# Two of a residual stream's additions as accumulating transfers within SBUF, in a four-layer graph network

## The chip, the cores and the metric

The kernel runs on one core of a Trainium2 chip. A core has five engines that run their own instruction queues and wait for each other by semaphores: TensorE (PE in the profile), VectorE (DVE), ScalarE (ACT), GpSimd (POOL) and SyncE (SP, which here only issues transfers). Sixteen DMA engines move data between HBM and SBUF and within SBUF. The metric is the device time of one execution in microseconds (us); less is better. Before the change it is 2353.62 us, the median of three runs from 2353.39 to 2353.85 us.

## The reference

There are 32 graphs of 512 nodes with 256 features. Each goes through four layers of the form x = x + layer(relu(layernorm(x)), adj), all in float32:

```python
# layer 0: att = softmax(h @ att_W @ h.T / 16 + mask)
#          y = tanh(att @ (h @ W0 + b0));  z = tanh(att @ (y @ W1 + b1));  x = x + z
# layer 1: e = leaky_relu(src + dst), masked; x = x + softmax(e) @ (h @ W.T)
# layer 2: e = exp(-leaky_relu(s + d)) where adj; x = x + elu(e @ (h @ W) / rowsum(e))
# layer 3: e = leaky_relu(h' a_12 h'.T + ...), masked; x = x + elu(h @ W_1 + (softmax(e) @ h) @ W_2)
```

The sums "x + z" of layer 0 and "x + elu(...)" of layer 2 are where the change lies. elu(v) is computed as relu(v) + min(exp(v), 1) - 1, so layer 2 has two additions to x per block.

## The kernel before

**Tiles.** A graph's x is one SBUF tile of 128 partitions by 4 blocks of 256 float32 (512 KB). Work on it goes in two halves, g = 0 and 1, of two blocks each: 128 x 512 elements, 256 KB. One graph at a time goes through the layers, but up to six graphs are in flight, each at another layer, so that PE always has matmuls of some graph to do. All big tiles share one pool of 34 "pages" of 4 KB per partition; the eight PSUM banks are shared too.

**The order.** It is written out by a planner inside the kernel (class `Plan`). Every step is registered with `op(engine, cost, after, emit, ...)`: its engine ("PE", "V" for DVE, "A" for ACT, "G" for GpSimd, "D" for transfers issued by SP), a pair of costs (how long it holds its engine, and after how long its result can be used), and what it comes after. `order` then lays the steps out by list scheduling: at each moment an engine takes the ready step with the earliest due time, where due times follow from the graph's number times a spacing and from the costs of what is still to come. A step with a `size` is booked with a shared wire instead: its bytes divided by 200 bytes per ns, plus 2000 ns. `best` tries 64 pairs of spacings and keeps one. The order that results is fixed in the program; on the chip each engine runs its queue strictly in that order and waits where a semaphore isn't there yet. The spacings chosen are 32000 and 8000 before, 34000 and 8000 after.

**Around layer 0's addition** (lines 936 to 952). For each half: eight matmuls give two blocks in one bank (`second_conv`, L936); two DVE instructions scale them and add the bias into z (`biased`, L940); ACT takes the tanh in place (`tanh2`, L944); DVE adds z to x (`add_z`, L947). Layer 1's normalisation (`normed`) starts from x: DVE takes statistics of each block (L557, L558), DVE and GpSimd make the factors (L561, L564, L567), ACT normalises (L571), the result goes through a transposing transfer issued by SP and back through ACT into hT (L591), and from there to PE.

**Around layer 2's additions** (lines 999 to 1018). For each block ACT writes exp into y2 (`lower`, L999) and relu into r2 (`upper`, L1002). For each half DVE adds min(y2, 1) to x (`add_lower`, L1009) and then r2 - 1 to x (`add_upper`, L1013). Layer 3's normalisation follows in the same way as above.

**GpSimd** does little: the reciprocal square roots for the normalisations (L564) and one 512 KB store per graph (L1154), which is a transfer issued from its queue. Its queue too is strictly in order.

Of the kernel before, what the change touches and what calls it, by code (L numbers as in the profile page):

```python
# [11 lines left out]
F32 = mybir.dt.float32  # L12
# [3 lines left out]
AF = mybir.ActivationFunctionType  # L16
ALU = mybir.AluOpType
PSUM = bass.MemoryType.PSUM

P = 128  # L20
# [13 lines left out]
def pe(n512=0, n258=0, n256=0, nt=0):  # L34
    t = n512 * PE512 + n258 * PE258 + n256 * PE256 + nt * PET
    return t, t + 170.0
# [3 lines left out]
V_MASK, V_CODE, V_HALF, V_PSUM, V_ADD = (602.0, 683.0), (600.0, 690.0), (600.0, 690.0), (395.0, 484.0), (334.0, 425.0)  # L40
A_COPY, A_HALF, A_PRELU, A_EXP, A_TANH = (477.0, 597.0), (253.0, 373.0), (570.0, 693.0), (519.0, 640.0), (373.0, 474.0)
A_BIAS, A_PRELU2 = (570.0, 687.0), (629.0, 722.0)
G_POW, G_STORE = (800.0, 850.0), (900.0, 900.0)
V_SUM, V_BLOCK = (334.0, 425.0), (790.0, 880.0)
A_HALF_BIAS = (345.0, 460.0)
A_NORM, A_JOIN, V_SPLIT = (491.0, 590.0), (620.0, 767.0), (332.0, 422.0)
# [160 lines left out]
def kernel(  # L207
# [31 lines left out]
    nc = tc.nc  # L239
    B, N, H = x.shape  # L240
# [9 lines left out]
    const = ctx.enter_context(tc.tile_pool(name="const", bufs=1))  # L250
# [69 lines left out]

    zero = const.tile([P, 1], F32, tag="zero", name="zero")
    nc.gpsimd.memset(zero, 0.0)
    one = const.tile([P, 1], F32, tag="one", name="one")
    nc.gpsimd.memset(one, 1.0)
    minus = const.tile([P, 1], F32, tag="minus", name="minus")
    nc.gpsimd.memset(minus, -1.0)

    def tile_of(name, cols, lines=HC):
        return const.tile([P, lines, cols], F32, tag=name, name=name)
# [7 lines left out]
    def raw(key, cols=H):  # L337
        return lambda: W[key][:, :, :cols]

    def load(dst, src, *keys):  # L340

        loads.append(prepare("G", G_LOAD, [], lambda: nc.gpsimd.dma_start(out=dst() if callable(dst) else dst, in_=src),
                             *keys, size=P * HC * H * 4 if keys else 4096))
        return loads[-1]

    def rows_of(w):
        return w.rearrange("(c p) k -> p c k", p=P)

    def load_column(t, v):

        return load(t, v.rearrange("(c p) -> p c", p=P))
# [5 lines left out]
    def halves(w):  # L357

        return w.rearrange("p c (i k) -> p c i k", i=2)[:, :, :, 1:]
# [19 lines left out]
    def product(dst, wT, rhs, cols, after, *keys):  # L379

        done = []
        for d in range(HC):
            key = f"bank{next(banks)}"

            def multiply(d, key):
                for c in range(HC):
                    nc.tensor.matmul(W[key][:, :cols], wT()[:, c, d * P : (d + 1) * P], rhs(c),
                                     start=(c == 0), stop=(c == HC - 1))

            def out_of(d, key):  # L390
                nc.vector.tensor_copy(dst(d), W[key][:, :cols])

            cost = pe(n256=2 * HC) if cols > P else pe(nt=2 * HC)
            a = prepare("PE", cost, after, partial(multiply, d, key), key, *keys)
            done.append(prepare("V", V_ADD, [a], partial(out_of, d, key), key, *keys))
        return done
# [28 lines left out]
    for n, dst, w, key in (("w0", w0_s, w0, "raw9"), ("att", att_s, att_w, "raw10")):  # L425
        ready[key] = [prepare("D", D_X, [], lambda w=w, key=key: nc.sync.dma_start(
            out=raw(key)(), in_=rows_of(w)), key, size=P * HC * H * 4)]
# [9 lines left out]
    a = [load(l1_sb, rows_of(l1_w), "raw0")]  # L437
# [5 lines left out]
    a = [load(lambda i=i: halves(l2_wide())[:, :, i, :], rows_of(l2_w)[:, :, i * HALF : (i + 1) * HALF], "raw12")  # L443
         for i in range(2)]
    t = transposed(lambda: halves(l2_wide()), l2_wt, a, "raw1", "raw12")
    a = t + [load_column(l2_ac, l2_a.rearrange("o n -> (o n)"))]
    a = a + product(lambda d: l2_wide()[:, d, :: HALF + 1], l2_wt,
                    lambda c: l2_ac.rearrange("p (o c) -> p c o", o=2)[:, c, :], 2, a, "raw1", "raw12")
# [3 lines left out]
    a = product(lambda d: awt()[:, d, :], a12_sb, lambda c: wt3()[:, c, :], H,  # L452
                t + [load(a12_sb, rows_of(l3_a12), "raw3")], "raw3", "raw4", "raw5")
    a = product(lambda d: m3_sb()[:, d, :], wt3, lambda c: awt()[:, c, :], H, a, "raw4", "raw5", "raw6")
# [4 lines left out]
    a = [load(lambda i=i: l3_wide()[:, :, i * (HALF + 1) : i * (HALF + 1) + HALF],  # L459
              rows_of(l3_w2)[:, :, i * HALF : (i + 1) * HALF], "raw8") for i in range(2)]  # L460
# [14 lines left out]
    def graph(b, adj_before, x_before):  # L475


        T = Tiles(b)

        def op(engine, cost, after, emit, *keys, size=0, weights=()):  # L480
            return plan.op(engine, cost, after, emit, b, T.uses(keys) + W.uses(weights), size)

        def two(g):
            return slice(2 * g, 2 * g + 2)
# [7 lines left out]
        def e(l, c):  # L492

            return T[f"e{l}_{c // 2}"][:, c % 2, :]
# [5 lines left out]
        def fetch_adj(t):  # L500
            nc.sync.dma_start(out=T["adj"][:, t, :], in_=adj[b, t * P : (t + 1) * P, :])


        got_x = [op("D", D_X, [x_before], partial(fetch_x, ts), "x", "ahead", size=P * H * 4 * (ts.stop - ts.start))
                 for ts in ([slice(t, t + 1) for t in range(NT)] if b == 0 else [slice(0, NT)])]
        got_adj = [adj_before]
        for t in range(NT):

            got_adj.append(op("D", D_ADJ, got_adj[-1:] if b else [], partial(fetch_adj, t), "adj", size=P * N * 4))
# [23 lines left out]
        for g in range(NT // 2):  # L533
            code = op("V", V_CODE, [got_adj[2 * g + 2], code], partial(classes, g), "adj", "code", "slot")
            for t in (2 * g, 2 * g + 1):
                if b:
                    coded.append(op("D", D_TURN, [code], partial(turn_code, t), "code", "codeT"))
                else:
                    key = f"bank_c{t}"
                    a = op("PE", pe(nt=NT), [code], partial(turn_code_pe, t, key), "code", key)  # L540
# [273 lines left out]
        if b == 0:  # L814

            qs, vs, es = [], [], []
            for k in range(HC):
# [7 lines left out]
                a = op("PE", pe(n512=4), hs + ready["raw10"], partial(features, k, key), key, "hT0", weights=["raw10"])  # L825
                qs.append(op("A", A_COPY, [a], lambda k=k, key=key: nc.scalar.copy(T["fa0"][:, k, :], T[key]), key, "fa0"))
            for t in range(NT):
# [7 lines left out]
                a = op("PE", pe(n256=4), [hs[t]] + ready["raw9"], partial(values, t, key), key, "hT0", weights=["raw9"])  # L835
                vs.append(op("V", V_ADD, [a], lambda t=t, key=key: nc.vector.tensor_add(
                    T["v0"][:, t, LEAD : LEAD + H], T[key][:, :H], b0_sb), key, "v0"))
            for c in range(NT):
                key = f"bank_q0{c}"

                def similar(c, key):
# [4 lines left out]
                a = op("PE", pe(n512=4), qs, partial(similar, c, key), key, "hT0", "fa0")  # L846
                a = op("A", A_COPY, [a], lambda c=c, key=key: nc.scalar.activation(
                    e(0, c), T[key], AF.Exp, scale=float(H) ** -0.5), key, f"e0_{c // 2}")
# [75 lines left out]
        a = None  # L924
        for c in range(NT):
            a = op("PE", pe(n512=4), [ys[c], a], partial(again, c), "bank_z0", "bank_z1", "y0", f"e0_{c // 2}")
        zs = [op("A", A_COPY, [a], partial(evacuate_z, k), f"bank_z{k}", "zT") for k in range(HC)]
        xs = []
        for g in range(NT // 2):
            key = f"bank_o{g}"  # L930

            def second_conv(g, key):
                for j in range(2):
                    t = 2 * g + j
                    for k in range(HC):
                        nc.tensor.matmul(T[key][:, j * H : (j + 1) * H], T["zT"][:, k, t * P : (t + 1) * P],  # L936
                                         w1_sb[:, k, :], start=(k == 0), stop=(k == HC - 1))

            def biased(t, key):
                nc.vector.scalar_tensor_tensor(T["z0"][:, t, :], T[key][:, t % 2 * H : (t % 2 + 1) * H],  # L940
                                               T["rs0"][:, t : t + 1], b1_sb, ALU.mult, ALU.add)

            def tanh2(g):
                nc.scalar.activation(T["z0"][:, two(g), :], T["z0"][:, two(g), :], AF.Tanh)  # L944

            def add_z(g):
                nc.vector.tensor_add(T["x"][:, two(g), :], T["x"][:, two(g), :], T["z0"][:, two(g), :])  # L947

            a = op("PE", pe(n256=8), zs + ready["w1"], partial(second_conv, g, key), key, "zT")
            bs = [op("V", V_PSUM, [a] + ready["b1"], partial(biased, 2 * g + j, key), key, "z0") for j in range(2)]  # L950
            a = op("A", A_EXP, bs, partial(tanh2, g), "z0")
            xs += [op("V", V_MASK, [a], partial(add_z, g), "z0", "x")] * 2


        def masked1(c):
# [20 lines left out]
        xs = attend(1, es, vs, second)  # L976
# [33 lines left out]

        def add_upper(g):
            xt = T["x"][:, two(g), :]
            nc.vector.scalar_tensor_tensor(xt, T["r2"][:, two(g), :], -1.0, xt, ALU.add, ALU.add)  # L1013

        us, xs = attend(2, es, vs, third), []
        for g in range(NT // 2):
            a = op("V", V_MASK, [u[0] for u in us[two(g)]], partial(add_lower, g), "y2", "x")
            xs += [op("V", V_MASK, [a] + [u[1] for u in us[two(g)]], partial(add_upper, g), "r2", "x")] * 2

# [73 lines left out]
        a = op("V", (334.0, 425.0), hi, highest, "crest3")  # L1095
        a = op("D", D_TURN, [a], partial(turn, 0, 2), "crest3")
        a = op("V", (900.0, 1000.0), [a], tops, "crest3")
        a = op("D", D_TURN, [a], partial(turn, 1, 0), "crest3")
# [29 lines left out]
            return op("V", V_PSUM, [a, wb[0, t // 2], wb[1, t // 2]], both_terms, key, "y3", "w3")  # L1128

        def upper3(ts):  # L1130
            nc.vector.scalar_tensor_tensor(T["x"][:, ts, :], T["y3"][:, ts, :], -1.0, T["x"][:, ts, :], ALU.max, ALU.add)

        def exp4(ts):
            nc.scalar.activation(T["r3"][:, ts, :], T["y3"][:, ts, :], AF.Exp, bias=one)

        def all_terms(ts):
            nc.vector.scalar_tensor_tensor(T["y3"][:, ts, :], T["r3"][:, ts, :], 1.0, T["x"][:, ts, :], ALU.min, ALU.add)
# [4 lines left out]
        us = attend(3, es, vs, fourth)  # L1142
        last = []
        for ts in parts(3):
            ts = slice(ts[0], ts[-1] + 1)
            whole = ts.stop - ts.start == 2
            u = op("V", V_MASK if whole else V_ADD, us[ts], partial(upper3, ts), "y3", "x")
# [13 lines left out]
    for b in range(B):  # L1161
        code, got = graph(b, code, got_x[-2])
        got_x.append(got)
# [37 lines left out]
```

## Time and profile before

| What | Value |
|---|---|
| Median of three runs | 2353.62 us |
| Span of the profiled execution | 2353.1 us |
| PE busy | 2328.9 us, 99% |
| DVE busy | 2099.7 us, 89% |
| ACT busy | 1719.9 us, 73% |
| POOL busy | 254.2 us, 11% |
| Transfers issued by POOL (queue q0) | 18.23 MB, 2.4% of the DMA engines' time |
| Transfers issued by SP (queue q1) | 157.51 MB, 31.2% of the DMA engines' time |
| 512 KB store issued by POOL, issue to landing, median | 3.6 us |

The profiled execution's span is 0.5 us below the median of the runs, so sums made against the span can be read against the median directly. The busy times are sums over instructions; DVE and ACT instructions that follow each other overlap by about 0.08 us in the records, so that a 0.68 us instruction takes 0.60 us of its engine's time from start to start. Idle time of an engine matters only if the engine that sets the end waits for it.

### The profile page before, as it was taken

The page shows a single profiled execution, that of the slowest core. Times are in us where ns is not written, and L with a number is a line of the kernel's source. Part 1 is how long each engine was busy: PE and PEld are TensorE (multiplying, and loading weights), DVE is VectorE, ACT ScalarE, POOL GpSimd, SP SyncE. Part 2 cuts the span into 40 slices and gives each one's busy share as a digit, 9 for nine tenths or more (in the row PEclk, how much of TensorE's full clock was granted, in tenths as well). Part 3 has the DMA queues.
Part 4 walks back from the last instruction along what each step waited for, and adds up shares of the span by engine and source line. Part 5 has one row for each costly group of instructions (what it writes and reads, how often), then busy time and mean ns, then how long its engine had stood idle before and what let it go on. Part 6 is the DMA issues. An engine that isn't in the chain of part 4 may idle for free.

```text
span 2353.1 us, 37623 instructions
## 1 busy us (share of the span) xinstructions
PE 2328.9 (99%) x12374; PEld 1992.0 (85%) x12374; DVE 2099.7 (89%) x6060; ACT 1719.9 (73%) x3421; POOL 254.2 (11%) x316
## 2 busy tenths in 40 slices
PE   8999999999999999999999999999999999999998
PEld 5789888888888888888898888888888888888887
DVE  8788899989889898898998889989898988987998
ACT  5677778767787677786777877677776778667874
POOL 3000101111011111011110010100101000010110
PEclk9999999999999999999999999999999999999999
DMA  7431233323333332333323334233343333321221
GB/s 192 106 78 28 57 79 79 88 66 83 72 75 84 78 83 66 70 88 90 82 58 74 80 85 90 54 82 70 88 91 68 86 68 73 86 54 33 55 49 42
DMA packets 429859, 178.26 MB, mean 76 GB/s; under 512 B 384128, under 2 KB 401664, under 8 KB 429664
## 3 DMA queue, kind: packets, MB, share of 16 engines
q1 hardware_dynamic: 424288, 157.51, 31.2%
q0 software_dynamic: 5232, 18.23, 2.4%
q8 instruction: 97, 1.59, 0.3%
q14 instruction: 98, 0.80, 0.1%
q10 hardware_dynamic: 144, 0.13, 0.0%
HBM read 67.64 MB, written 16.89 MB: 36 GB/s over the span
## 4 chain that ended last, share of the span: by engine, by line
PE 94%; DVE 4%; DMA 1%; ACT 1%; issue 0%; POOL 0%; DVEq 0%; ACTq 0%
PE bank_a L758 36%; PE bank_z L918 9%; PE bank_s3p L1040 5%; PE bank_o L936 4%; PE bank_q0p L874 4%; PE bank_f3p L783 4%; PE bank_w3p L809 4%; PE bank_v0p L809 4%; PE bank_f0p L783 4%; PE bank_s3q L1040 3%; PE bank_q0q L874 3%; PE bank_v1p L809 2%; PE bank_v3p L809 2%; PE bank_v2p L809 2%; PE bank_v3q L809 2%; PE bank_v1q L809 2%
## 5 line engine op out<-in xcount | busy, mean ns | idle before, releaser
L758 PE MATMUL bank_a<-v,e 128*128 128x258 f32 (+2 forms) x4096 | 1017.7, 381 | 0.9 <-DVE e L956 0.9
L758 PEld LDWEIGHTS bank_a<-v,e 128*128 128x128 f32 x4096 | 744.1, 190 | 108.9 <-issue 18.2
L591 ACT COPY hT<-planesT 128x512 uint16<-128x512 uint16 x508 | 377.8, 769 | 93.9 <-DMA planesT<-planes 93.2
L564 POOL TENSOR_TENSOR rstd<-ve,mhalf 128x2 f32<-128x2 f32 x256 | 216.0, 863 | 1732.3 <-DVE ve L561 1599.4
L571 ACT ACTIVATE xn<-x,off,rstd 128x256 f32<-128x256 f32 x512 | 278.0, 593 | 39.8 <-DVE off L567 38.9
L918 PE MATMUL bank_z<-e,y 128*128 128x512 f32 x512 | 240.8, 593 | 0.0
L557 DVE BATCH_NORM_STATS2 st<-x 128x6 f32<-128x256 f32 x512 | 210.5, 411 | 3.8 <-DMA x<-in_x_dram 3.8
L576 DVE COPY planes<-xn 128x512 uint16<-128x512 uint16 x380 | 156.4, 420 | 17.3 <-DMA planesT<-planes 10.2
L882 ACT ACTIVATE e<-e 128x512 f32<-128x512 f32 x124 | 77.8, 629 | 121.9 <-DVE e L893 61.8
L732 ACT ACTIVATE e<-row,v 128x512 f32<-128x512 f32 x224 | 156.6, 719 | 0.8 <-DMA row<-row 0.7
L735 ACT ACTIVATE e<-e 128x512 f32<-128x512 f32 x256 | 157.1, 630 | 0.0
L918 PEld LDWEIGHTS bank_z<-e,y 128*128 128x128 f32 x512 | 92.7, 190 | 64.9 <-issue 60.5
L695 ACT COPY v<-bank_v1p 128x258 f32<-128x258 f32 x128 | 47.7, 373 | 120.0 <-PE bank_v1p L809 119.3
L936 PE MATMUL bank_o<-w_sb,zT 128*128 128x256 f32 x512 | 118.5, 379 | 0.2 <-ACT zT L922 0.2
L1047 DVE SCALAR_TENSOR_TENSOR e<-bank_s3p,v,mask 128x256 f32<-128x256 f32 x256 | 111.0, 475 | 8.4 <-PE bank_a L758 4.4
L558 DVE BATCH_NORM_AGGREGATE mv<-st 128x2 f32<-128x6 f32 x512 | 93.2, 182 | 17.5
L936 PEld LDWEIGHTS bank_o<-w_sb,zT 128*128 128x128 f32 x512 | 95.8, 190 | 12.8 <-ACT zT L922 0.6
L664 DVE TENSOR_TENSOR hs<-hT,hs 128x256 f32<-128x256 f32 x254 | 105.1, 414 | 1.1
L667 DVE TENSOR_TENSOR hs<-hT 128x512 f32<-128x512 f32 x127 | 86.6, 682 | 14.5 <-ACT hT L591 14.3
L1086 ACT ACTIVATE e<-e,zero 128x512 f32<-128x512 f32 x128 | 88.2, 721 | 12.9 <-DVE crest L1064 11.4
L885 DVE TENSOR_TENSOR e<-bank_q0p,mask 128x512 f32<-128x512 f32 x124 | 84.5, 682 | 13.8 <-PE bank_q0p L874 12.3
L1089 DVE TENSOR_TENSOR e<-e,crest 128x512 f32<-128x512 f32 x128 | 85.9, 682 | 8.3 <-ACT crest L1083 8.1
(202 smaller groups left out, 4891.3 us busy)
## 6 DMA issues: line engine op xcount, KB each, us to landing
adj<-in_adj_dram SPq DMA_DIRECT2D x128, 256.0 KB
x<-in_x_dram SPq DMA_DIRECT2D x31, 512.0 KB
out_dram<-y POOLq DMA_DIRECT2D x31, 512.0 KB, 3.6
row<-row SPq DMA_DIRECT2D x56, 256.0 KB
planesT<-planes SPq DMA_TRANSPOSE x508
codeT<-code SPq DMA_TRANSPOSE x124
crest<-crest SPq DMA_TRANSPOSE x64
row<-sT SPq DMA_DIRECT2D x56, 2.0 KB
```

Of the source, the lines that this page charges most:

```text
L557: nc.vector.bn_stats(T[f"st{l}"][:, t, :], T["x"][:, t, :])
L564: nc.gpsimd.tensor_tensor(T[f"rstd{l}"][:, two(g)], T[f"ve{l}"][:, two(g)], mhalf[:, two(g)], ALU.pow)
L571: nc.scalar.activation(T[f"xn{l}"][:, t, :], T["x"][:, t, :], AF.Relu, bias=T[f"off{l}"][:, t : t + 1], scale=T[f"rstd{l}"][:, t : t + 1])
L591: nc.scalar.copy(bits[:, :, :, t * P : (t + 1) * P], T[f"planesT{l}_{t}"].rearrange("p (b c) n -> p b c n", b=2))
L735: nc.scalar.activation(e(l, c), e(l, c), AF.Exp, scale=sign)
L758: nc.tensor.matmul(T[key][:, : LEAD + H + 1 - lead], e(l, c)[:, t * P : (t + 1) * P], T[f"v{l}"][:, c, lead:], start=(c == 0), stop=(c == ...
L783: nc.tensor.matmul(p[:, : N // 2], w[:, x - 1, :], right(x), start=fresh, stop=True, skip_group_check=True)
L809: nc.tensor.matmul(p[:, j * k : (j + 1) * k], right(x)[:, j * P : (j + 1) * P], w[:, x - 1, :], start=fresh and j == 0, stop=True, skip_gr ...
L874: nc.tensor.matmul(p[:, j * N // 2 : (j + 1) * N // 2], right(x)[:, j * P : (j + 1) * P], left(x), start=fresh and j == 0, stop=True, skip ...
L918: nc.tensor.matmul(T[f"bank_z{k}"], T["y0"][:, c, k * P : (k + 1) * P], e(0, c), start=(c == 0), stop=(c == NT - 1))
L936: nc.tensor.matmul(T[key][:, j * H : (j + 1) * H], T["zT"][:, k, t * P : (t + 1) * P], w1_sb[:, k, :], start=(k == 0), stop=(k == HC - 1))
L1040: nc.tensor.matmul(p[:, j * N // 2 : (j + 1) * N // 2], left(x)[:, j * P : (j + 1) * P], right(x), start=fresh and j == 0, stop=True, skip ...
```

## The change

In graphs 1 to 29 (graph 0 and the last two, `ends`, keep the DVE instructions), layer 0's addition and the second addition of layer 2 are no longer DVE instructions but transfers issued by GpSimd from SBUF to SBUF, each of 256 KB, with an operation that adds what is read to the destination. To the planner they are steps of engine "G" that hold it for 900 ns and have a size of 256 KB. The -1 of layer 2's elu, which the DVE instruction added on its way, is left out of x there; x is then larger by 1 everywhere until layer 3 takes it back: layer 3's normalisation doesn't see a constant, and the constants of its last terms (the bias of w3, the limit in `upper3` and the bias of the exp) change from -1, -1, 1 to -2, -2, 2. These constants change no instruction's shape. In graphs 0, 30 and 31 `add_upper` becomes a plain DVE addition of the same size.

```diff
-G_POW, G_STORE = (800.0, 850.0), (900.0, 900.0)
+G_POW, G_STORE, G_SUM = (800.0, 850.0), (900.0, 900.0), (900.0, 4500.0)
...
-    one = const.tile([P, 1], F32, tag="one", name="one")
-    nc.gpsimd.memset(one, 1.0)
-    minus = const.tile([P, 1], F32, tag="minus", name="minus")
-    nc.gpsimd.memset(minus, -1.0)
+    minus, plus = (const.tile([P, 1], F32, tag=n, name=n) for n in ("minus", "plus"))
+    nc.gpsimd.memset(minus, -2.0)
+    nc.gpsimd.memset(plus, 2.0)
...
+        ends = b < 1 or b >= B - 2
+        summed = ("V", V_MASK) if ends else ("G", G_SUM)
...
             def add_z(g):
-                nc.vector.tensor_add(T["x"][:, two(g), :], T["x"][:, two(g), :], T["z0"][:, two(g), :])
+                if ends:
+                    nc.vector.tensor_add(T["x"][:, two(g), :], T["x"][:, two(g), :], T["z0"][:, two(g), :])
+                else:
+                    nc.gpsimd.dma_start(out=T["x"][:, two(g), :], in_=T["z0"][:, two(g), :], accum_op=ALU.add)
...
-            xs += [op("V", V_MASK, [a], partial(add_z, g), "z0", "x")] * 2
+            xs += [op(*summed, [a], partial(add_z, g), "z0", "x", size=0 if ends else 2 * P * H * 4)] * 2
...
         def add_upper(g):
             xt = T["x"][:, two(g), :]
-            nc.vector.scalar_tensor_tensor(xt, T["r2"][:, two(g), :], -1.0, xt, ALU.add, ALU.add)
+            if ends:
+                nc.vector.tensor_add(xt, xt, T["r2"][:, two(g), :])
+            else:
+                nc.gpsimd.dma_start(out=xt, in_=T["r2"][:, two(g), :], accum_op=ALU.add)
...
-            xs += [op("V", V_MASK, [a] + [u[1] for u in us[two(g)]], partial(add_upper, g), "r2", "x")] * 2
+            xs += [op(*summed, [a] + [u[1] for u in us[two(g)]], partial(add_upper, g), "r2", "x", size=0 if ends else 2 * P * H * 4)] * 2
...
-            nc.vector.scalar_tensor_tensor(T["x"][:, ts, :], T["y3"][:, ts, :], -1.0, T["x"][:, ts, :], ALU.max, ALU.add)
+            nc.vector.scalar_tensor_tensor(T["x"][:, ts, :], T["y3"][:, ts, :], -2.0, T["x"][:, ts, :], ALU.max, ALU.add)
...
-            nc.scalar.activation(T["r3"][:, ts, :], T["y3"][:, ts, :], AF.Exp, bias=one)
+            nc.scalar.activation(T["r3"][:, ts, :], T["y3"][:, ts, :], AF.Exp, bias=plus)
```

In the built program, GpSimd's queue of a graph in the middle then runs: a transfer of layer 2 (half 0), two square roots of another graph, a transfer of layer 2 (half 1), two square roots, both transfers of layer 0 one after the other, three square roots, the store of an older graph and one more square root. As costs and steps have changed, the planner has laid out all engines' queues anew: PE's queue holds the same matmuls in another sequence.

## The prediction

> **What bounds the kernel now.** I read the page's busy times and the chain of work first, then the stages, then who waits for whom.
>
> ```profile
> span 2353.1 us, 37623 instructions
> PE 2328.9 (99%) x12374; PEld 1992.0 (85%) x12374; DVE 2099.7 (89%) x6060; ACT 1719.9 (73%) x3421; POOL 254.2 (11%) x316
> PE 94%; DVE 4%; DMA 1%; ACT 1%; issue 0%; POOL 0%; DVEq 0%; ACTq 0%
> ```
>
> The first two lines say that PE idles 24.2 us in all; the third, from the chain that ended last, says that the chain is PE from end to end. The stages show where the 24.2 us lie (columns: stretch, its length, busy us of PE, weight loads, DVE, ACT, POOL, granted clock, DMA share, GB/s):
>
> ```profile
> 0.00:50.00 50.00, 40.98 (x167) 27.71 (x168) 38.45 (x144) 28.27 (x53) 19.97 (x41) 1.00 0.82 206
> 50.00:100.00 50.00, 48.74 (x249) 39.62 (x248) 43.35 (x117) 30.23 (x57) 1.37 (x2) 1.00 0.52 116
> ...
> 900.00:1200.00 300.00, 299.86 (x1606) 258.46 (x1605) 271.68 (x788) 225.96 (x452) 32.15 (x38) 1.00 0.34 75
> ...
> 2100.00:2250.00 150.00, 148.18 (x820) 126.75 (x819) 130.48 (x369) 116.09 (x235) 14.46 (x16) 1.00 0.23 47
> 2250.00:2300.00 50.00, 46.06 (x240) 40.13 (x239) 47.60 (x145) 40.47 (x85) 6.29 (x7) 0.97 0.24 48
> 2300.00:2353.00 53.00, 46.61 (x266) 41.48 (x264) 46.63 (x108) 27.34 (x50) 1.51 (x2) 0.98 0.16 45
> ```
>
> From 100 to 2100 us PE is without gaps (299.86 of 300; the clock is 1.00). That its busy time there is work and not stretched by waiting shows in the timeline: twelve 259-column matmuls take 2.62 us, 0.218 us each, wherever they stand, and the same group of matmuls (L936) comes back after 288.2 us for four graphs each time, 72.05 us per graph. Of the idle time, 8.8 us pass before the first matmul, and 6.5 us after the last; no edit here touches these. Left are 8.9 us of stalls: 1.5 up to 100 us, 1.6 in the 2000 us of the middle, 1.8 from 2100 to 2250 and 3.9 from 2250 to 2300. **The change can gain 8.9 us (0.4%) at most, and only at the ends.** DVE's 89% is no bound: in the middle it is busy 271.7 of 300 us, and PE doesn't wait for it.
>
> **What the Trainium skill says.** "DMA: Bandwidth & Descriptors" (Anatomy of one DMA — SWDGE (gpsimd) path) prices a transfer issued by GpSimd at 2.0 us plus its bytes over 436 GB/s. For the 512 KB store that gives 3.2 us; the trace has 3.6, a tenth more (the view of line 1154's instructions: min/median/max of the issue in ns, then of the landing):
>
> ```profile
> L1154 POOL DMA_DIRECT2D out_dram<-y x31: 752/790/1347, 279.6 to 2345.4; - x31
> ...
> DMA to landing us min/median/max: 3.4/3.6/4.8
> ```
>
> "Collectives: The Full Stack" (The bandwidth ceiling: the fold count and why AG ≠ RS ≠ AR) says that an add in the DMA engines costs two source reads, not cycles of the adder; no run here shows that yet. "SBUF — State Buffer" (Who interferes with whom) says that a DVE copy in its two-port mode keeps GpSimd from writing descriptors; the spread of the issue, 790 ns to 1347 ns, agrees with such a delay of 0.56 us but doesn't name its cause.
>
> **The change part by part.**
>
> *Removed:* two halves of two additions in 29 graphs, 58 + 58 DVE instructions. In the groups by shape (busy us, mean ns of one, idle before it):
>
> ```profile
> L1013 DVE SCALAR_TENSOR_TENSOR x<-r,x 128x512 f32<-128x512 f32 x64 | 43.6, 681 | 0.3
> L947 DVE TENSOR_TENSOR x<-x,z 128x512 f32<-128x512 f32 x64 | 43.6, 682 | 0.4 <-ACT z L944 0.4
> ```
>
> 58 x 0.682 + 58 x 0.681 = 79.1 us, so DVE falls to about 2021 us (86%). On the path this is worth nothing in the middle, since PE covers it; cover gone, it would be 116 x 0.60 = 70 us. The constants are free: no instruction changes its shape.
>
> *Added on POOL:* 116 issues. At the store's 0.79 us they are 92 us, POOL 346 us (15%). Hidden: POOL idles over 2000 us. Its queue is in order, though: square roots (L564) now stand behind transfers that wait for a tanh or for add_lower. In the built order the roots behind a transfer are mostly of steps that come later anyway, and a root 0.8 us late holds one DVE instruction (L567); I cost it at 0, up to 0.8 us twice per graph if ACT's tanh is late.
>
> *Added on the DMA engines:* 116 x 256 KB = 30.4 MB written, with two reads each. The trace has no accumulating transfer. If it moves as the 512 KB store does (as many bytes read), queue q0 grows from 2.4% to about 9% of the engines' time, beside 31% for SP's transposes and loads. The store disturbs nothing in the middle already, so 0.
>
> *The new wait:* the statistics (L557) now wait for a landing instead of a DVE instruction just before. Everything depends on the time L from issue to landing. Lower bound: a plain 256 KB copy by the skill's price, 2.0 + 0.26/0.436 = 2.6 us. Upper bound: 6.3 us, the slowest 256 KB load issued by POOL in this trace, with the DMA engines 82% busy. I take 3.6 us, the store's, as 512 KB are read. The planner books 262144/200 + 2000 ns = 3.3 us, so it has put other DVE work between; how much, I count in the changed kernel's DVE queue, with durations of the trace less 0.08 us overlap. Behind `add_lower`: 4.6 us (even graphs) and 5.9 us (odd) for the first half, 4.0 and 3.9 us for the second. Behind the second `biased`: 5.0 us (even) and 6.2 us (odd) for the first half, 5.1 and 5.8 us for the second, but tanh comes out of this. The timelines of ACT and of DVE for one graph before (start us, us):
>
> ```profile
> 677.71 0.63 ACT L944 ACTIVATE z<-z 128x512 f32<-128x512 f32 x1
> 680.35 0.64 ACT L944 ACTIVATE z<-z 128x512 f32<-128x512 f32 x1
> ```
>
> ```profile
> 676.24 0.88 DVE L940 SCALAR_TENSOR_TENSOR z<-bank_o,rs,b_sb 128x256 f32<-128x256 f32 x2 [0.24 <-PE bank_o L936]
> 678.23 0.87 DVE L940 SCALAR_TENSOR_TENSOR z<-bank_o,rs,b_sb 128x256 f32<-128x256 f32 x2
> ```
>
> In this graph tanh ends 1.2 us (678.34 - 677.12) and 1.9 us (680.99 - 679.10) after. Left for the transfer are 3.8 to 5.0 us and 3.2 to 3.9 us. With L = 3.6 only one of these eight places is short, by 0.4 us. What stands behind the waiting DVE instruction are evacuations and masks of other graphs that PE waits for; but PE came back to a bank 1.2 us after DVE had read it in one example (L885 ends 618.08, PE writes again at 619.30), so I take about 1 us as absorbed. Cost in the middle: 0 to 2 us in all for places with less margin, I take 1.
>
> *The ends:* the start (graph 1's additions) and the last graphs are newly laid out. I take 0 for them, -7 to +9 as the range from the rivals below.
>
> Sum against the profiled execution: 2353.1 + 1 + 0 = 2354; the median is 0.5 above that span, so 2354.5.
>
> **The rivals.**
>
> *B, the landing is late (slower).* At L = 4.2 us five of the eight places fall short, the worst by the 1 us that is absorbed; from there it decides. At L = 5.2 the worst shortfalls are 2.0 us (layer 0) and 1.2 us (layer 2) in even graphs and 1.3 us twice in odd ones; the second half's wait mostly contains the first's. With 1 us absorbed each, that is 1.2 and 0.6 us, a mean of 0.9 us x 29 graphs = 26 us: 2380. At L = 6.3 it is 3.1 us x 29 = 90 us: 2444. For it: two reads, 31% of DMA time already taken, the 4.8 us of the slowest store, and a queue order laid out for 3.3 us. Against it: DVE has 9% idle time, and the waits have other work before them.
>
> *C, the ends get shorter (faster).* From 2250 to 2300 us DVE is busy 47.6 of 50 us while PE loses 3.9 us. Graphs 26 to 29, the last of the changed ones, lose 16 x 0.60 = 9.6 us of DVE work, some of it there. If this removes two thirds of the 8.9 us of stalls, 6 us: 2348. Against it: the last two graphs, which alone run at the very end, keep their DVE additions.
>
> *D, the ends get worse (slower).* In the changed PE queue graph 30's second convolution (L936) stands 12 us of PE work later than before, with its two remaining layers squeezed against the end, and graph 1's additions now depend on transfers while the DMA engines are 52 to 82% busy. If the 5.7 us of stalls after 2100 doubled and the start lost 2 us: 2361.
>
> That the change does nothing is excluded: the built queue of POOL has the 116 transfers.
>
> **How the numbers follow.** A (hidden) 0.41, with its own range 2350 to 2358; B 0.31; C 0.17; D 0.11. Predicted is A's 2354.5. A measurement of this kernel tells 0.2%, 4.7 us, from no change. Faster: most of C, 0.14; within: A and the rest of C, 0.43; slower: B and most of D, 0.43. For 8 in 10 the range runs from 2347 (leaving out a third of C) to 2395 (leaving out the upper third of B, where L is beyond 5.5 us).
>
> **What would show it.** DVE's busy time near 2021 us and POOL's near 346 show the removal and the issues. The landing time of the two new transfer lines decides between A and B: at or below 4.2 us, PE must still be at 299.8 of 300 us in the middle, and the L936 groups 72.05 us per graph apart; above, DVE idle time must appear before L557 with a DMA as releaser, and PE waits for DVE or ACT in the middle. C and D show as PE busy time after 2100 us and before 150 us. I am wrong if PE's pace in the middle changes with landings under 4 us (then POOL's in-order queue or the transposes, delayed by the new traffic, would be the place to look), or if the ends move by more than 9 us.

## The result and the profile after

The changed kernel takes 2378.65 us, the median of four runs from 2376.83 to 2379.72; the kernel before, 2353.51 us (four runs, 2353.25 to 2353.85). The ratio is 1.0105, 95% interval 1.0091 to 1.0119: slower by about 25 us. The profiled execution's span is 2377.8 us, 24.7 us above that of before. The page of the changed kernel (busy times of the engines, the transfers issued by GpSimd, the chain of work that ended last):

```profile
span 2377.8 us, 37854 instructions
PE 2339.2 (98%) x12374; PEld 1991.3 (84%) x12374; DVE 2030.0 (85%) x5944; ACT 1719.9 (72%) x3421; POOL 350.2 (15%) x432
...
q0 software_dynamic: 21936, 48.64, 10.3%
...
PE 76%; ACT 8%; DMA 7%; DVE 6%; issue 3%; SPq 0%; POOL 0%; DVEq 0%; ACTq 0%; POOLq 0%
```

DVE has lost its 70 us, POOL has gained its 96, and neither is what counts: the chain, which was PE for 94% of its length, now passes through transfers, ACT and DVE for 21%. Of its 175 us in transfers, 103 are the two new ones (54.5 us x<-r, 48.9 us x<-z). The 24.7 us are found twice in PE's line. Its idle time has grown from 24.2 us to 38.6 (2377.8 - 2339.2), which is 14.4; and its busy time from 2328.9 to 2339.2, which is 10.3, though it does the same 12374 matmuls. A matmul's record lasts about 0.38 us where the next one starts 0.22 us after it, so a delay of up to 0.16 us lengthens "busy" and shows as no idle time.

The stages of the changed kernel (stretch, its length, busy us of PE, weight loads, DVE, ACT and POOL, granted clock, DMA share, GB/s):

```profile
0.00:50.00 50.00, 40.67 (x167) 27.91 (x168) 38.92 (x148) 29.36 (x54) 19.97 (x41) 1.00 0.80 210
50.00:100.00 50.00, 47.98 (x244) 38.22 (x242) 39.47 (x102) 26.90 (x50) 2.68 (x3) 1.00 0.52 117
...
900.00:1200.00 300.00, 298.58 (x1592) 256.16 (x1591) 258.32 (x753) 222.89 (x445) 46.11 (x54) 1.00 0.46 93
...
1500.00:1800.00 300.00, 295.21 (x1569) 252.62 (x1568) 257.67 (x754) 219.93 (x439) 43.79 (x52) 1.00 0.43 89
...
2100.00:2250.00 150.00, 149.22 (x789) 126.25 (x787) 123.52 (x369) 108.69 (x215) 19.10 (x24) 1.00 0.26 54
2250.00:2300.00 50.00, 46.91 (x262) 40.95 (x262) 46.42 (x135) 41.91 (x90) 5.93 (x8) 1.00 0.27 53
```

The middle, full before (299.86 of 300 us), now has gaps everywhere, and in most stretches PE also gets fewer matmuls done (1592 instead of 1606 from 900 to 1200 us). The start is a little worse than before, the end a little better. To count both kinds of delay I took from the trace, for successive matmuls, the time from start to start above what is usual for the same line and tile. By this count PE loses 19.7 us before and 44.6 after, a difference of 24.9, which is the span's. In parts, 3.5 becomes 30.7 us between 100 and 2100 us, 4.8 becomes 5.4 up to 100 us, and 11.4 becomes 8.5 after 2100 us. **The loss is all in the middle: 27 us; start and end together give back 2 to 3.**

The two new transfers, x<-z of layer 0 and x<-r of layer 2 (min/median/max of the issue in ns, then of the time from issue to landing):

```profile
L952 POOL DMA_DIRECT2D x<-z x58: 847/893/1319, 98.9 to 2077.4; - x58
...
DMA to landing us min/median/max: 3.3/3.8/6.3
```

```profile
L1021 POOL DMA_DIRECT2D x<-r x58: 852/903/1343, 221.8 to 2273.4; - x58
...
DMA to landing us min/median/max: 3.3/4.2/6.0
```

And who waits in the changed kernel (engine, its line, what it waits for: us in total, times, longest):

```profile
ACT xn L573 <- DVE off L569: 76.7, 60, 6.0
...
DVE st L559 <- DMA x<-r: 26.1, 25, 2.0
...
DVE st L559 <- DMA x<-z: 16.4, 23, 2.0
...
DVE off L569 <- POOL rstd L566: 8.1, 26, 0.9
...
PE bank_f3p L785 <- DVE hs L666: 5.9, 7, 2.4
```

DVE waits 42.5 us for landings, in 48 places, up to 2.0 us. It stands before the statistics (L559), as the prediction said it would if the landing came late. At each of these places GpSimd had begun the issue before DVE became free: the sum's inputs were there, and what DVE still waited for was the landing. How such a wait reaches PE is seen at one place, in layer 0 of one graph. The second half's tanh ends at 1857.58 us, and GpSimd issues the transfer from 1857.88. DVE's timeline then (start us, us, instruction, and in brackets its idle time before and what ended it):

```profile
1860.47 0.68 DVE L961 SCALAR_TENSOR_TENSOR e<-codeT,e 128x512 f32<-128x512 bf16 x1
1861.07 0.41 DVE L800 TENSOR_TENSOR fa<-fa,bank_f0p 128x256 f32<-128x256 f32 x1
1861.40 0.69 DVE L669 TENSOR_TENSOR hs<-hT 128x512 f32<-128x512 f32 x1
1862.87 0.43 DVE L559 BATCH_NORM_STATS2 st<-x 128x6 f32<-128x256 f32 x1 [0.79 <-DMA x<-z]
1863.34 0.18 DVE L560 BATCH_NORM_AGGREGATE mv<-st 128x2 f32<-128x6 f32 x1
1863.43 0.39 DVE L666 TENSOR_TENSOR hs<-hT,hs 128x256 f32<-128x256 f32 x1
```

and PE's:

```profile
1862.27 1.04 PE L760 MATMUL bank_a<-v,e 128*128 128x259 f32 x4
1863.97 0.67 PE L785 MATMUL bank_f3p<-hs,m 128*128 128x256 f32 x2 [0.67 <-DVE hs L666]
```

DVE is free at 1862.09 and goes on at 1862.87, 5.0 us after the issue began. Two places behind the waiting statistics stands L666, a combination of feature blocks for another graph's matmul L785. It runs 0.79 us late, and PE starts 0.83 us late by the count above: the whole wait comes through. The same place comes back in other graphs (PE starts L785 late by 1.01, 1.10, 0.77, 0.84 and 0.83 us at 407, 1278, 1570, 1717 and 1864 us).

This is layer 0, and it is not so everywhere. In the 5 us after each wait between 100 and 2100 us PE is late by 13.2 us in all behind layer 0's waits (16.4 us), but by 3.5 us behind layer 2's (24.2 us), of which some 2.4 us would be met there by chance (the mean over the same stretches moved by 10 to 60 us); behind 17 of layer 2's 24 waits it is not late at all. So layer 0's waits come through for the most part, and layer 2's, which are as long and longer, hardly. What PE loses later than 5 us after a wait can't be tied to a single one.

### The profile page after: what moved, and what is told of

Read it like the earlier page. It is cut to its first block, busy times and chain, and to the rows that moved or that the text cites. A ratio compares the mean times of both kernels' runs of the same rounds, so it can differ in the third digit from the quotient of the medians.

```text
span 2377.8 us, 37854 instructions
## 1 busy us (share of the span) xinstructions
PE 2339.2 (98%) x12374; PEld 1991.3 (84%) x12374; DVE 2030.0 (85%) x5944; ACT 1719.9 (72%) x3421; POOL 350.2 (15%) x432
## 3 DMA queue, kind: packets, MB, share of 16 engines
q0 software_dynamic: 21936, 48.64, 10.3%
## 4 chain that ended last, share of the span: by engine, by line
PE 76%; ACT 8%; DMA 7%; DVE 6%; issue 3%; SPq 0%; POOL 0%; DVEq 0%; ACTq 0%; POOLq 0%
PE bank_a L760 31%; PE bank_z L920 6%; PE bank_q0p L876 4%; PE bank_s3p L1048 4%; PE bank_f3p L785 4%; PE bank_v0p L811 3%; PE bank_w3p L811 3%; PE bank_q0q L876 3%; PE bank_o L938 3%; PE bank_f0p L785 2%; PE bank_s3q L1048 2%; PE bank_v3p L811 2%; DMA x<-r 2%; DMA x<-z 2%; PE bank_v3q L811 2%
## 5 line engine op out<-in xcount | busy, mean ns | idle before, releaser
L760 PE MATMUL bank_a<-v,e 128*128 128x258 f32 (+2 forms) x4096 | 1018.6, 382 | 7.9 <-ACT e L1100 6.1
L760 PEld LDWEIGHTS bank_a<-v,e 128*128 128x128 f32 x4096 | 743.7, 190 | 105.7 <-ACT e L1100 9.3
L566 POOL TENSOR_TENSOR rstd<-ve,mhalf 128x2 f32<-128x2 f32 x256 | 207.9, 827 | 967.7 <-DVE ve L563 949.4
L573 ACT ACTIVATE xn<-x,off,rstd 128x256 f32<-128x256 f32 x512 | 285.1, 600 | 80.7 <-DVE off L569 76.7
L559 DVE BATCH_NORM_STATS2 st<-x 128x6 f32<-128x256 f32 x512 | 212.1, 414 | 47.5 <-DMA x<-r 26.1
L952 POOL DMA_DIRECT2D x<-z x58 | 51.4, 886 | 434.8 <-ACT z L946 404.6
L666 DVE TENSOR_TENSOR hs<-hT,hs 128x256 f32<-128x256 f32 x254 | 105.7, 416 | 0.7
L1094 ACT ACTIVATE e<-e,zero 128x512 f32<-128x512 f32 x128 | 87.7, 718 | 24.9 <-DVE crest L1072 24.9
```

The costliest lines, as they stand in the source:

```text
L559: nc.vector.bn_stats(T[f"st{l}"][:, t, :], T["x"][:, t, :])
L566: nc.gpsimd.tensor_tensor(T[f"rstd{l}"][:, two(g)], T[f"ve{l}"][:, two(g)], mhalf[:, two(g)], ALU.pow)
L573: nc.scalar.activation(T[f"xn{l}"][:, t, :], T["x"][:, t, :], AF.Relu, bias=T[f"off{l}"][:, t : t + 1], scale=T[f"rstd{l}"][:, t : t + 1])
L760: nc.tensor.matmul(T[key][:, : LEAD + H + 1 - lead], e(l, c)[:, t * P : (t + 1) * P], T[f"v{l}"][:, c, lead:], start=(c == 0), stop=(c == ...
```

## The experiments

The theory to be tested is that the loss is the late landing: DVE waits for it, and what stands behind DVE's waiting instruction is late for PE. Its rivals are that the newly laid out order (or the spacing that came with it) is worse by itself, and that the new traffic or GpSimd's queue disturbs others. In the diffs a minus is the changed kernel, unless the text says "before". Each figure is a median; its ratio to the kernel before, measured beside it, follows with the interval.

**1. The new order, with the additions back on DVE.** The order of every engine is that of the changed kernel; at the places of the transfers, DVE instructions are emitted instead.

```diff
-                if ends:
+                if True:
                     nc.vector.tensor_add(...)   # in add_z, and likewise in add_upper
```

> Every engine's queue is laid out as in the changed kernel (the planner still books the 116 additions as transfers of GpSimd), but the additions are emitted as DVE instructions at the same places. Theory T (the sum lands later than the order allows for): PE is full again between 100 and 2100 us, and the time is 2354 us, within 5. Rival O (the new order itself loses the time, whoever adds): about 2378 us, with PE still losing some 20 us in the middle. Rival Q (the added transfers disturb GpSimd's queue or SP's transposes): 2354 us too, as there are no transfers.

Measured: 2371.96 us, 1.0078 (1.0063 to 1.0093). This missed what the theory of the late landing expected, and taken alone it speaks for the order. But its waits show what it really tested (PEld are the weight loads ahead of the matmuls):

```profile
PEld bank_a L760 <- DVE e L961: 20.5, 38, 0.9
...
PE bank_a L760 <- DVE e L961: 6.0, 15, 0.5
```

PE now waits for masks (L961) that stand on DVE a few places behind the added instructions, which the order hadn't planned there. Of the 22.6 us that PE loses in the middle, 19.1 are late starts of L760. So 116 instructions of 0.60 us on DVE, 70 us in all and each unplanned, cost about 18 us: a quarter comes through. It isn't a clean test of the order, which needs the additions gone (experiment 7); but it shows that half a microsecond on DVE at a wrong place can cost PE as much.

**2. The transfers alone, off the path.** The kernel before, with its DVE additions, and 116 accumulating transfers of the same size beside them, each of a tile that is no longer needed onto itself. The planner knows of them; only the page's next user waits for them.

```diff
+        def aside(key, g):
+            nc.gpsimd.dma_start(out=T[key][:, two(g), :], in_=T[key][:, two(g), :], accum_op=ALU.add)
...
             xs += [op("V", V_MASK, [a], partial(add_z, g), "z0", "x")] * 2
+            if 0 < b < B - 2:
+                op("G", G_SUM, xs[-1:], partial(aside, "z0", g), "z0", size=2 * P * H * 4)
```

> The kernel before, with its DVE additions, and behind each of the 116 an accumulating transfer of the same size that adds a dead tile (z0 or r2, after its last use) to itself; nobody waits for it but the next user of its page. T: 2354 us, within 5: the transfers cost nothing where nothing waits for them. Q: 2365 us or more, with ACT waiting longer for the transposes (90 us in both kernels so far) or DVE for GpSimd's square roots. O says nothing here.

Measured: 2357.21 us, 1.0015 (1.0008 to 1.0022). The issues and the traffic as such cost about 3.4 us (2 to 5 by the interval), not 25.

**3 and 4. One of the two sums alone.** In experiment 3 only layer 0's addition is a transfer, in 4 only layer 2's. The planner lays each out anew (spacing 34000).

```diff
-            if ends:
+            if True:
                 nc.vector.tensor_add(xt, xt, T["r2"][:, two(g), :])
...
-            xs += [op(*summed, [a] + [u[1] ...], partial(add_upper, g), "r2", "x", size=...)] * 2
+            xs += [op("V", V_MASK, [a] + [u[1] ...], partial(add_upper, g), "r2", "x")] * 2
```

> Only layer 0's addition is a transfer (58 of them); layer 2's is the DVE instruction. T: the DVE waits for the landing of layer 0's sums were 16 of 42 us, so about 0.4 of the 25 us: 2363 us, 2357 to 2369. O: anything between 2354 and 2378, not tied to the waits. Q: half of the transfers, so about half of the loss, 2366 us.

> Only layer 2's second addition is a transfer (58 of them); layer 0's is the DVE instruction. T: waits of 26 of 42 us, and the matmuls of layer 3's features were the ones that came late most, so about 0.6 of the 25 us: 2369 us, 2362 to 2375. Q: half, 2366 us. O: not tied to the waits.

Measured: 2362.24 us, 1.0036 (1.0023 to 1.0049), for layer 0 alone, and 2360.34 us, 1.0030 (1.0019 to 1.0040), for layer 2 alone. Either sum costs something, and 8.5 and 6.6 us do not add up to the 25 of both. In the first the landing takes 4.6 us and DVE waits 32.8 us for it; in the second 3.4 us and 6.4 us. PE loses 12.8 us more in the middle than before in the first, 9.5 in the second (the ends give some of it back). In the second that is more than DVE waited for landings, so a part of it has another source, the order or the traffic. How much of a DVE wait reaches PE thus depends on where the order has put it, and these two runs, with other orders each, can't say more.

**5 and 6. The landing booked later.** If the landing is later than the planner believes, tell it so: 2500 ns more, and in the next 4500 ns more, for these steps when the order is laid out (1000 ns more in the estimate that chooses the spacing).

```diff
-                        until = wire - now + self.LAND + o["late"]
+                        until = wire - now + self.LAND + o["late"] + o.get("order_more", 0.0)
...
+                o["order_more"], o["replay_more"] = 2500.0, 1000.0
```

> The changed kernel; the planner books each of the 116 sums as landing 2.5 us later when it lays out the order (5.8 us instead of 3.3) and 1.0 us later when it compares spacings. Nothing else differs. T: the DVE waits for landings fall from 42 us to under 10, PE loses under 5 us in the middle, and the time is 2350 to 2358 us. O and Q: the transfers and a new order are still there, so 2365 us or more.

> As the run before with 4.5 us instead of 2.5 us (7.8 us in the order). T: no further gain in the middle, since the slowest landing was 6.3 us and the issue comes 0.3 to 0.5 us after its inputs; a longer chain per graph costs at the ends at most: 2350 to 2360 us. O and Q: 2365 us or more.

Measured: 2384.39 us, 1.0135 (1.0119 to 1.0150), with 2500 ns (spacing 36000), and 2370.77 us, 1.0076 (1.0059 to 1.0093), with 4500 ns (spacing 34000). DVE's waits for landings are gone in both (0.8 us in the first, none in the second), and the loss is not. Both missed what the theory of the late landing expected. Experiment 12 comes back to it.

**7. The new order without the sums.** The changed kernel with the two transfers left out in graphs 1 to 29, every engine's other instructions as they are. x lacks the two sums there.

```diff
-                    nc.gpsimd.dma_start(out=T["x"][:, two(g), :], in_=T["z0"][:, two(g), :], accum_op=ALU.add)
+                    pass
...
-                nc.gpsimd.dma_start(out=xt, in_=T["r2"][:, two(g), :], accum_op=ALU.add)
+                pass
```

> The changed kernel with its order, but in graphs 1 to 29 the two additions are left out altogether (no transfer, no DVE instruction), so the residual lacks them. Theory T2 (the late landings, 3.3 to 6.3 us after an issue that itself comes 0.3 to 0.5 us late, make the changed order's 27 us): PE loses at most 6 us between 100 and 2100 us, and the time is 2351 us, within 5. Rival O2 (the changed order loses the time by itself): PE loses 15 us or more in the middle, 2362 us or more.

Measured: 2351.88 us, 0.9993 (0.9985 to 1.0002). The stages of that kernel, columns as above:

```profile
900.00:1200.00 300.00, 300.00 (x1602) 258.61 (x1600) 263.13 (x776) 227.68 (x454) 31.48 (x38) 1.00 0.35 75
...
1500.00:1800.00 300.00, 298.84 (x1595) 257.00 (x1594) 261.58 (x767) 218.25 (x438) 31.10 (x38) 1.00 0.35 78
```

PE is full again, to within about a microsecond. With the sums and every wait for them gone, the new order loses nothing; what experiment 1 saw was its lack of room on DVE.

**8 and 9. The spacing.** The planner chose 34000 instead of 32000. Experiment 8 is the kernel before (all on DVE) with 34000, experiment 9 the changed kernel with 32000.

```diff
-        apart = min(itertools.product(self.APART, self.APART_LAST), key=lambda a: self.replay(self.order(pools, *a)))
+        apart = 34000.0, 8000.0
```

> The kernel before with nothing changed but the planner's spacing, fixed at 34000 and 8000, the pair that it chose for the changed kernel. O2 by way of the spacing: 2360 us or more. T2: an order with no transfers has no reason to lose, 2350 to 2358 us.

> The changed kernel with the spacing fixed at 32000 and 8000, the pair of the kernel before. O2 by way of the spacing: 2350 to 2360 us. T2: the landings are as late as ever, 2365 us or more.

Measured: 2354.92 us, 1.0006 (0.9997 to 1.0014), for the first: not told from no change, so the spacing isn't it. The second takes 2459.66 us, 1.0453 (1.0438 to 1.0469). Among its waits:

```profile
DVE st L559 <- DMA x<-r: 32.4, 30, 2.1
PE bank_a L760 <- DVE e L961: 28.7, 15, 3.7
```

The DVE waits for landings are about as long as in the changed kernel (46.0 us), but in this order PE loses 106 us in the middle, about 16 of them in short stretches in which only half of the clock was granted.

**10. The transfers in the old order.** The kernel before, all engines in its order; only where DVE would add, GpSimd issues the transfer (with the constants of the change). No step has been moved to make up for the landing.

```diff
             xs += [op("V", V_MASK, [a], partial(add_z, g), "z0", "x")] * 2
...
-                nc.vector.tensor_add(T["x"][:, two(g), :], T["x"][:, two(g), :], T["z0"][:, two(g), :])
+                nc.gpsimd.dma_start(out=T["x"][:, two(g), :], in_=T["z0"][:, two(g), :], accum_op=ALU.add)
```

> The order of the kernel before on every engine (the planner books the additions as DVE instructions of 0.68 us), but the 116 additions are emitted as transfers at the same places, with the constants of the changed kernel. T2: each landing comes 3 to 5 us later than the order has it, and DVE waits at nearly every one of the 116, some 150 to 300 us in all before other idle time is taken off: 2400 us or more. O2: the order is the good one, so at most 2370 us.

Measured: 2549.77 us, 1.0826 (1.0807 to 1.0845). The waits between 300 and 2100 us:

```profile
DVE st L557 <- DMA x<-r: 118.8, 41, 4.7
...
DVE st L557 <- DMA x<-z: 97.4, 34, 5.0
```

216 us of DVE waits there, and PE loses 169 us in the same stretch. Not all of that is waiting: about 28 us fall into short stretches in which only half of the clock was granted. From 900 to 1200 us the mean granted clock is 0.97, where the changed kernel has 1.00 (in its whole middle it has one such stretch, of 3.4 us, worth 1.7 of its 27 us; columns as above):

```profile
900.00:1200.00 300.00, 283.59 (x1463) 238.84 (x1464) 240.76 (x711) 198.02 (x397) 44.84 (x50) 0.97 0.38 80
```

The re-laid order of the changed kernel takes away seven eighths of the time lost; what is left of DVE's waits is the part of the landing that it didn't cover.

**11. The same order and the same transfers, but no one waits for the landing.** The changed kernel again, every instruction in its place on every engine; only each transfer adds its source tile to itself instead of to x. x lacks the two sums in graphs 1 to 29, and the statistics don't wait. Only the tile's page does.

```diff
-                    nc.gpsimd.dma_start(out=T["x"][:, two(g), :], in_=T["z0"][:, two(g), :], accum_op=ALU.add)
+                    nc.gpsimd.dma_start(out=T["z0"][:, two(g), :], in_=T["z0"][:, two(g), :], accum_op=ALU.add)
...
-                nc.gpsimd.dma_start(out=xt, in_=T["r2"][:, two(g), :], accum_op=ALU.add)
+                nc.gpsimd.dma_start(out=T["r2"][:, two(g), :], in_=T["r2"][:, two(g), :], accum_op=ALU.add)
```

> The changed kernel with every engine's order as it is, and with the same 116 transfers of 256 KB issued from the same places of GpSimd's queue; only each of them adds its source tile to itself, a tile that no one reads afterwards, instead of to x. So x lacks the two sums in graphs 1 to 29, and the statistics on DVE wait for no landing, while the traffic, the issues and the pages' release stay. Against the same order without any transfers (2351.9 us). Theory L (it is the landings that are waited for which cost): 2352 to 2356 us, PE busy 299 of 300 us in the middle. Theory Q (traffic, or GpSimd's queue and the square roots in it, cost in this order what they did not in the old one): 2368 us or more, with DVE and ACT waits for rstd and for planesT as in the changed kernel.

Measured: 2357.30 us, 1.0017 (1.0010 to 1.0023). The landings take as long as in the changed kernel for layer 0 (3.8 us) and nearly so for layer 2 (3.9 us); here the stages are:

```profile
900.00:1200.00 300.00, 299.74 (x1595) 257.87 (x1594) 262.68 (x774) 226.65 (x453) 45.48 (x54) 1.00 0.44 89
...
1500.00:1800.00 300.00, 298.97 (x1601) 257.36 (x1600) 261.24 (x763) 220.68 (x440) 44.09 (x52) 1.00 0.44 91
```

This is the run that decides. It is a little above the 2352 to 2356 of theory L and far from the 2368 of theory Q. Between it and the changed kernel lies who depends on the transfer, and that is worth 21.3 us (2378.65 - 2357.30); by PE's count it is 20.8 us in the middle (30.7 against 9.9). Above experiment 7 it stands by 5.4 us: the issues and the traffic in this order. GpSimd's queue is cleared of suspicion too: between 300 and 2100 us DVE waits 4.8 us for the square roots here and without any transfers, 4.9 in the changed kernel.

Two things besides the wait for the landing differ. The statistics no longer wait for tanh or relu either, which stand ahead of the transfer; in the changed kernel, though, each transfer that DVE waited for had been issued before DVE was free. And layer 2's transfer doesn't wait for `add_lower` here, so some are issued earlier. What that is worth of the 21 us, no run separates.

**12. The later booking, without the sums.** Experiment 6 with the two transfers left out in graphs 1 to 29, as in 7.

> The kernel whose landings are booked 4500 ns later (2370.8 us) with the order of all engines as it is there, but the two transfers left out in graphs 1 to 29: x lacks these sums there. In that kernel no DVE instruction waited for a landing any more and it was 17 us slower than before all the same. Theory O (an order laid out for a longer chain is worse by itself: more graphs in flight, pages and steps squeezed elsewhere): 2366 us or more without the transfers too. Theory M (the transfers delay what SP issues, above all the transposes that ACT waits for): 2350 to 2355 us, with ACT's waits for planesT back near 68 us in 300 to 2100 us from 116.

Measured: 2359.08 us, 1.0022 (1.0014 to 1.0030). It lies between the two theories. That order costs 5.4 us by itself, where the changed kernel's costs nothing; with its transfers it costs about 12 us more (2370.77), though DVE waits for none of them. ACT's wait for the transposed planes between 300 and 2100 us, without the transfers and then with them:

```profile
ACT hT L598 <- DMA planesT<-planes: 81.2, 54, 5.7
```

```profile
ACT hT L598 <- DMA planesT<-planes: 116.0, 82, 5.7
```

35 us more, of which some must be transposes that start later behind a later x, and some may be transposes slowed by the traffic. In the changed kernel's order the traffic alone was worth 5.4 us; the other 6 us or so have no run that names them. So booking the landing later removes the wait from DVE, and the time is lost elsewhere; where, is only in part known. Why the booking of 2500 ns is worse still (PE waits 13.5 us there for ACT, before the matmuls that are L785 in the changed kernel) stays open.

None of these kernels is faster than the one before beyond the noise.

## Why the prediction was right or wrong

The range held the time, but the likeliest case, A, was wrong, and rival B, "the landing is late", is what happened, close to its price: 2380 against 2378.65 us. The range held because B had a share in it, not because A's working was right, and that B's price came so close is luck, as shown below.

- **The bound and the 8.9 us to gain.** Right. PE is the busiest engine in every run, and even with the sums left out altogether (experiment 7) the gain was under 2 us, and its interval takes in none.
- **What is removed and added.** Right: DVE 2030.0 us (2021 said; 2030.3 in experiment 7, so the 9 us more come with the order, not with the transfers), POOL 350.2 (346), q0 10.3% of the engines' time (about 9). An issue takes 0.89 to 0.90 us, not the store's 0.79; 116 of them make 12 us more on an idle engine.
- **GpSimd's queue and the traffic at 0.** The queue was right. The traffic was not quite free: 3.4 us (experiment 2) and 5.4 us (experiment 11, above 7), against "so 0". A store per graph that disturbs nothing was no proof for four transfers more.
- **L = 3.6 us.** This is the first step that failed. The medians are 3.8 and 4.2 us, and up to 6.3. Before them comes a hop that the sum left out: from the end of the last input to the start of the issue, 0.30 us behind tanh and 0.53 us behind `add_lower` or the relu (medians of the trace). So DVE's cover had to hold 4.1 and 4.7 us in the middle case, not 3.6, and the eight places counted held between 3.2 and 5.9. The Trainium skill ("Collectives: The Full Stack", The bandwidth ceiling: the fold count and why AG ≠ RS ≠ AR) has an add in the DMA engines read two sources, which makes 512 KB of an accumulating 256 KB. From its price ("DMA: Bandwidth & Descriptors", Anatomy of one DMA — SWDGE (gpsimd) path) the estimate for 512 KB is 3.2 us. The fastest landings, 3.3 us, agree with two reads. So does queue q0, whose share grew by 7.9% of the engines' time for 30.4 MB more, where 2.4% had moved 18.2 MB, though packets slowed by other traffic would raise it too. The store's median, which I took as the typical value, is close to the fastest landing here and below the typical one.
- **"I take about 1 us as absorbed", and the middle at 0 to 2.** This is the second step that failed, and it is the worse one. It came from one example on another bank, and it took no account of what stands directly behind the statistics. In the timeline above 0.79 us on DVE are 0.83 us on PE. By the prediction's rule, the 15 waits over 1 us in the changed kernel would have cost their excess, 6.9 us in all; they and the shorter ones cost 21. That is about half of DVE's 42.5 us of waiting, and one allowance for all places hides how it comes about: as far as the 5 us behind each wait show, a fifth is absorbed in layer 0 and nearly everything in layer 2, up to 2 us. DVE's idle 9% is not slack where a mask or a feature block is due next.
- **Rival B's price.** Right in mechanism; right in sum by luck, through two errors that cancel: it reached 26 us with landings of 5.2 us and 1 us absorbed each; the real landings were about a microsecond shorter at the median, and less was absorbed. Its threshold of L = 4.2 us took one L for all transfers. The landings spread: 66 of the 116 were no longer than 4.2 us, but 34.4 of the 42.5 us of waiting stand behind the longer ones.
- **Rivals C and D.** Start and end together moved by 2 to 3 us in C's direction; whether by C's mechanism, no run separates. Of D only 0.6 us at the start is seen.
- **What would show it.** The test named there separated A from B "at 4.2 us". The measured landings, 3.8 and 4.2, lie on A's side of it while everything else (DVE idle before the statistics with a transfer as releaser, PE late for DVE in the middle) showed B. A threshold on the median can't tell A from B when the landings spread from 3.3 to 6.3 us; the signs were right.

## What to carry to other kernels

Moving an addition from a busy engine to a transfer swaps 0.6 us of an engine for 4 to 5 us of latency, so price the place: count, at each place, from the end of the last input (hop included) to the first instruction that needs the sum, against the slow landings and not the median of another transfer. Then read what stands behind the waiting instruction in its queue: if the bottleneck engine takes it next, nearly all of the wait can come through, as in the timeline of layer 0 here; if not, a wait of 1 to 2 us can vanish, as in layer 2. And to find what such a change costs, keep the order and turn the transfer aside, so that it is issued and moved but no one waits for it; the difference is what the dependency costs.

## What the runs showed of the hardware

The same 256 KB accumulating transfer lands after 3.3 us in the best case, and its median goes from 3.4 us (experiment 4, layer 2) to 5.2 us (experiment 5, layer 0) by where the order puts it. The packets in the trace say beside what. Count, from issue to landing, the share of the 16 DMA engines' time that packets of SP's queue held. In the changed kernel the few transfers with less than a tenth (4 of layer 0, 3 of layer 2) landed after 3.4 and 3.3 us at the median, those with 0.3 to 0.5 after 4.8 us (14 transfers) and 4.2 us (30). In experiment 5's layer 0 the figures are 3.3 us under a tenth (4) and 5.6 us above 0.3 (51). This is a correlation (0.6 for layer 0 and 0.8 for layer 2 in the changed kernel), and no run varied SP's transposes by themselves. I had not expected that transfer engines busy for only a third of the time would spread the landings by 3 us.
